# New pools for attention's tiles, other places for the next stage's first tiles, and another queue for their loads, in a two-layer metaformer on one core

## The chip, the cores and the metric

The kernel runs on one core of a Trainium2 chip. A core has five engines that run their own instruction streams and wait for each other by semaphores: TensorE (PE in the profile, its weight loads PEld), VectorE (DVE), ScalarE (ACT), GpSimd (POOL) and SyncE (SP). DMA transfers are issued from the streams of SP, ACT and POOL and are carried by 16 DMA engines. The metric is the device time of one execution in microseconds (us), the median of several runs. All data are float32.

## The reference

Four images of 384 channels and 32 x 32 positions go through two layers. Cut to what matters:

```python
x = x + attention(ln_c(x), w_qkv, w_proj, b_proj, table_q, table_k, table_v)   # 8 heads of 48
t = tokens(x)
t = t + gelu(ln(t) @ kron(c_fc_1, c_fc_2).T) @ kron(c_proj_1, c_proj_2).T
x = image(t)
x = x + convolutions(ln_c(x))          # depthwise 7x7, 5x3, 3x5, 7+7 and 5+5 separable
t = tokens(x)
t = t + mixture(ln(t), 4 experts, top 2)   # hidden 1536
x = image(t)

def attention(...):                    # n = 1024 positions; idx = clipped relative offset, 15 x 15
    a = q @ k.T * s + take(q @ table_k, idx) * s + take(k @ table_q, idx).T * s
    a = softmax(a)
    out = a @ v + scatter(a, idx) @ table_v
    return out @ w_proj + b_proj
```

## The kernel before

The kernel is written with a tile framework: a tile is taken from a pool, a pool has its place in the on-chip memory (SBUF), and the framework sets the semaphores. Pools that are opened one after the other are laid one above the other. When a stage's pools are closed, those of the next stage take the same memory, and the first instruction of each engine that uses a new pool waits for whatever still uses memory that the pool overlaps. This wait goes by pool: a tile that shares nothing with an old tile waits all the same if its pool does. The framework also orders each engine's stream; instructions passed through `pin` (`tc.keep_in_program_order`) keep the order in which they are written.

Three stages follow each other.

1. `qkv_phase` (L133) takes 512 positions at a time, eight in all. It writes `qk_d` (queries and keys) and `v_d` (values) to DRAM with DMAs that POOL issues (L179, L193). The last `v_d` store is 1 MB.

2. `attention_phase` (L199) runs over eight heads. For each head `prepare` (L294) multiplies the keys and the queries of one image column with the position tables, 32 rows in pairs: `product` gives `tabq_ps`, which ScalarE copies into a tile `st` (L318, three buffers of two rows), which SP stores in DRAM as `sd` (L319), and `tabk_ps`, which VectorE transposes into the key table `b2` (L314). For the first head nothing else goes on meanwhile. Then `fetch` (L334) reads a row of `sd` back as `s1`, and POOL adds it to a part of `b2` (L349) to make `bias`. Then come, over 32 rows of queries, scores, exponentials, transposes into `aT`, windows into `a1t`, and the products with the values `vb` and the value table `tvw`. The results go to DRAM as `ao_d`, in two halves of 16 image rows (L501), when `rd` and its spread copies `rb` (L489) have given the softmax's denominators. At the end of the last head stand `values`, four `value_table` products (`tv_ps`), `normalise` of two groups (one on VectorE, one on POOL) and `store` (L654 to L659). Before the change the pool `a_fixed` holds `vb`, `aT`, `a1t`, `tvw`, `b2` and, above these, `arow`, `extra`, `zero`, `den` and `tvs`, which are cleared by memsets when attention begins (L251 to L267). `b2` is the largest, 60 KB in each partition.

3. `rest_phase` (L902) does the projection, both feed-forward parts and the convolutions, image by image. It loads constants in three packs, on ScalarE's queue (`const`, L933): `pack0` has the projection's weights, `pack1` the first feed-forward's, among them `fold`, `pack2` the convolutions' and the gate's. `loads` (L961) brings the two halves of an image: `at` from `ao_d` and `xs`, a half of `xb`, from the input. For image 0, `at` and `xs` of half 0, then `xs` and `at` of half 1 are issued by SP. At L1441 `fold` is scaled by VectorE and centred (`sum_ps`, L128). `project` (L979) multiplies `at` with `pack0` in three chunks of 128 channels (`proj_ps`, L985) and adds to `xb` (L988), for half 0 and then for half 1; `token_stats` follows each time with `row_ps` and the statistics, `net` with the feed-forward part. The experts' first weights `w00` and `w01` are loaded on SP by `preload` (L1113) after image 0's halves, and then image 1's `xb`. `img` is cleared by POOL (L1457).

Before the change the three packs, `img` and `w` lie at the bottom of the memory (`r_w`), `xb` in `r_x` above, and `at` in `r_work`, which also holds `xc` and `scale`.

Of the kernel before, what the change touches and what calls it, by code (L numbers as in the profile page):

```python
# [11 lines left out]
F32 = mybir.dt.float32  # L12
# [6 lines left out]
P = 128  # L19
B, C, IMG = 4, 384, 32  # L20
N = IMG * IMG
NT = B * N
KC = C // P
HEADS, HD = 8, C // 8
SCALE = HD ** -0.5
MAXD = 7
SPAN = 2 * MAXD + 1
ZW = 2 * IMG - 1
NBLK = N // P
PADR = 6  # L30
AROWS = IMG + 2 * PADR
YB = 4
YT = 16
XT = 8
VW = 64
# [4 lines left out]
TOK = 512  # L40
# [27 lines left out]
WIDTHS = [sum(m for _, m in p) for p in PACKS]  # L68


def bcast(ap, dim, n):

    dims = [list(d) for d in ap.ap]
    dims[dim] = [0, n]
    return bass.AP(ap.tensor, ap.offset, dims)


def token_stats(nc, pools, ident, x, eps, rows=None, step=4):


    small, psum, tag = pools
    nj = x.shape[2] // P
    mv = small.tile([P, nj, 2], F32, tag=f"s_mv{nj}", name="s_mv")
    for j in range(nj):
        ps = psum.tile([P, TOK], F32, tag=tag, name="row_ps")
        for k in range(KC):
            nc.tensor.transpose(ps[:, k * P : (k + 1) * P], x[:, k, j * P : (j + 1) * P], ident)
        st = small.tile([P, 6], F32, tag="s_st", name="s_st")
        nc.vector.bn_stats(st, ps[:, :C])
        nc.vector.bn_aggr(mv[:, j, :], st)  # L90
        if rows is not None:
            nc.scalar.copy(rows[j], ps[:, :C])
        if j % step == step - 1:
            yield 0.7 * step, 0.45 * step
    rstd = small.tile([P, nj, 1], F32, tag=f"s_rstd{nj}", name="s_rstd")
    nc.scalar.activation(rstd, mv[:, :, 1:2], AF.Sqrt, bias=eps)
    nc.vector.reciprocal(rstd, rstd)
    return mv[:, :, 0:1], rstd


def result(steps):

    while True:
        try:
            next(steps)
        except StopIteration as end:
            return end.value


def to_partitions(nc, pools, ident, one, values):  # L110

    small, psum, tag = pools
    nj = values.shape[1]
    dg = small.tile([P, nj, P], F32, tag="s_dg", name="s_dg", bufs=1)
    nc.vector.tensor_tensor(dg, bcast(ident.unsqueeze(1), 1, nj), bcast(values, 2, P), ALU.mult)
    ps = psum.tile([P, TOK], F32, tag=tag, name="all_ps")
    nc.tensor.matmul(ps, one, dg.rearrange("p j n -> p (j n)"), start=True, stop=True)
    return ps


def center(nc, psum, tag, one, w):

    n = w.shape[2]
    for c in range(0, n, C):
        part = w[:, :, c : min(c + C, n)]
        ps = psum.tile([P, part.shape[2]], F32, tag=tag, name="sum_ps")
        for k in range(KC):
            nc.tensor.matmul(ps, one, part[:, k, :], start=(k == 0), stop=(k == KC - 1))  # L128
        for k in range(KC):
            nc.vector.scalar_tensor_tensor(part[:, k, :], ps, -1.0 / C, part[:, k, :], ALU.mult, ALU.add)  # L130
# [68 lines left out]
def attention_phase(tc, cst, held, tabs, tv, qk_d, v_d, ao_d, xs_d, heads):  # L199
# [15 lines left out]
    nc = tc.nc  # L215
# [14 lines left out]

    with ExitStack() as es:
        dram = es.enter_context(tc.tile_pool(name="a_dram", bufs=2, space=DRAM))
        fixed = es.enter_context(tc.tile_pool(name="a_fixed", bufs=1))
        work = es.enter_context(tc.tile_pool(name="a_work", bufs=2))
        small = es.enter_context(tc.tile_pool(name="a_small", bufs=4))
# [2 lines left out]
        ps_o = es.enter_context(tc.tile_pool(name="a_ps_o", bufs=1, space=PSUM))  # L238

        ident = cst["ident"]  # L240
        vb = fixed.tile([P, B, NBLK, VW], F32, name="vb")
        aT = fixed.tile([P, NBLK, YB, P], F32, name="aT")
        a1t = fixed.tile([P, 4, IMG, YT, B], F32, name="a1t")
        tvw = fixed.tile([P, 4, IMG, HD], F32, name="tvw")
        b2 = fixed.tile([P, SPAN, IMG, IMG], F32, name="b2")

        NA = 3
        arow, extra = [], []
        for i in range(NA):
# [3 lines left out]
            x = fixed.tile([P, 4, IMG], F32, name=f"extra{i}")  # L253
# [15 lines left out]
        def load_tables(h, bulk=bulk):  # L269
            for lo, i, r0 in ((64, 0, h * HD), (0, 1, C + h * HD)):  # L270
                bulk(tab[lo : lo + HD], tabs[i, h])
                yield
                for b in range(B):
                    dst, src = kq[lo : lo + HD], qk_d[r0 : r0 + HD, b * N : (b + 1) * N]
                    if lo:
                        dst = dst.rearrange("p (y b x) -> p b y x", y=IMG, b=B)[:, b]
                        src = src.rearrange("p (y x) -> p y x", x=IMG)
                    else:
                        dst = dst[:, b * N : (b + 1) * N]
                    bulk(dst, src)  # L280
                    yield
# [260 lines left out]
        for n, h in enumerate(heads):  # L542
# [27 lines left out]
            loads = iter(()) if last else load_tables(heads[n + 1])  # L570
# [331 lines left out]
def rest_phase(tc, cst, x, ao_d, ins, xs_d, y_d, x2_d, out):  # L902
# [7 lines left out]
    nc = tc.nc  # L910
    ident, one = cst["ident"], cst["one"]
    with ExitStack() as es:
        wp = es.enter_context(tc.tile_pool(name="r_w", bufs=1))
        xp_ = es.enter_context(tc.tile_pool(name="r_x", bufs=2))
        ld = es.enter_context(tc.tile_pool(name="r_ld", bufs=2))
        work = es.enter_context(tc.tile_pool(name="r_work", bufs=2))
        hid = es.enter_context(tc.tile_pool(name="r_hid", bufs=4))
        small = es.enter_context(tc.tile_pool(name="r_small", bufs=2))
# [5 lines left out]
        def pin(ins_):  # L924
            return tc.keep_in_program_order(ins_)
# [5 lines left out]
        packs = {}  # L931

        def const(name, shape):  # L933
            pack, at = PLACES[name]
            if pack not in packs:
                packs[pack] = wp.tile([P, WIDTHS[pack]], F32, name=f"pack{pack}")
                pin(nc.scalar.dma_start(packs[pack], ins[f"pack{pack}"]))
            n = int(np.prod(shape[1:]))
            t = packs[pack][:, at : at + n]
            if len(shape) == 3:  # L940
                t = t.rearrange("p (a b) -> p a b", b=shape[2])
            if len(shape) == 4:
                t = t.rearrange("p (a b c) -> p a b c", b=shape[2], c=shape[3])
            return t

        wproj = const("w_proj", [P, KC, C])
        bproj = const("b_proj", [P, KC])
        cf2 = const("c_fc_2", [P, KC])
        fold = const("fold", [P, KC, P])
        c1t = const("c_fc_1", [P, NF // 4, P])  # L950
# [6 lines left out]
        pc = {"before": const("before", [P, P]), "blocks": const("blocks", [P, MAXB]), "wrow": const("wrow", [P, 2])}  # L957
        pc["one"], pc["slot0"] = one, const("slot0", [P, NEXP])
        img = wp.tile([P, KC, IMG + 6, IMG + 6], F32, name="img")

        def loads(b, xb):  # L961

            ats = []
            for half in range(2):
                at = work.tile([P, KC, TOK], F32, tag="xc", name="at")
                xs = xb[:, :, half * TOK : (half + 1) * TOK]
                pair = [
                    (at, ao_d[half][:, b].rearrange("(k p) n -> p k n", p=P)),
                    (xs, x[b, :, half * TOK : (half + 1) * TOK].rearrange("(k p) n -> p k n", p=P)),
                ]  # L970
                for dst, src in pair[::-1] if half and not b else pair:
                    ins_ = nc.sync.dma_start(dst, src)
                    if not b:
                        pin(ins_)
                ats.append(at)
                yield 0.0, 0.0
            return ats

        def project(xs, at):  # L979

# [62 lines left out]
        def halves_of(xb):  # L1043
            return [xb[:, :, half * TOK : (half + 1) * TOK] for half in range(2)]
# [14 lines left out]
        def normalise(xb, halves, which=range(2)):  # L1059

            for half in which:
                xs = xb[:, :, half * TOK : (half + 1) * TOK]
                mean, rstd = yield from token_stats(nc, stp, ident, xs, cst["eps6"])
                mps = to_partitions(nc, (small, ps_m, "m"), ident, one, mean)
                sps = to_partitions(nc, (small, ps_m, "m"), ident, one, rstd)
                scale_sb = work.tile([P, TOK], F32, tag="scale", name="scale")
                nc.scalar.copy(scale_sb, sps)
                xc = work.tile([P, KC, TOK], F32, tag="xc", name="xc")
                nc.vector.tensor_tensor(xc, xs, bcast(mps.unsqueeze(1), 1, KC), ALU.subtract)
                halves.append((xc, scale_sb))  # L1070
                yield 3.0, 2.0
# [41 lines left out]
        def preload(w, keep=lambda ins_: ins_, which=range(2)):  # L1113
            for fh in which:
                keep(nc.sync.dma_start(w[fh], ins["w12"][fh * P : (fh + 1) * P, :]))
# [266 lines left out]
        xbs, marks = {}, {}  # L1382
# [58 lines left out]
        for k in range(KC):  # L1441
            nc.vector.tensor_scalar_mul(fold[:, k, :], fold[:, k, :], cf2[:, k : k + 1])
        center(nc, ps_m, "m", one, fold)
        xbs[0] = xp_.tile([P, KC, N], F32, name="xb", tag="xb")
        xs0, xs1 = halves_of(xbs[0])
        halves = [[] for _ in range(B + 1)]
        at0, at1 = result(loads(0, xbs[0]))
        preload(wts[0], pin)
        rstd0 = result(project(xs0, at0))
        rstd1 = result(project(xs1, at1))  # L1450
# [152 lines left out]
```

## Time and profile before

| | us |
|---|---|
| median of three runs | 3050.28 |
| lowest and highest | 3049.36, 3055.75 |
| the profiled execution | 3065.37 |
| its span, first instruction to last | 3063.6 |
| TensorE busy in it | 2923.0 (95%) |
| VectorE busy | 1960.3 (64%) |
| ScalarE busy | 1369.9 (45%) |
| GpSimd busy | 1150.8 (38%) |
| the stage of QKV ends (last `v_ps` product) at | 216.1 |
| attention's last product (`tv_ps`) ends at | 1484.0 |

The profile's times are those of one execution and count from its first instruction. A chain of waits is followed back from the last instruction: at each step to what released it, or to the instruction before it on its engine. In the timeline a line has start, length, engine, source line, operation, tiles and shapes, how many were merged, and in square brackets how long the engine was idle before and what ended that. A releaser is inferred from the semaphore that came last by the profile; where several DMAs landed together, the name can be that of a neighbour. Engine "SPq" or "ACTq" marks the issue of a DMA, not its transfer.

### The profile page before, as it was taken

Reading aid. Unit: us, or ns where it says so; the run is one execution under the profiler, and the core shown is the slowest. Engines: PE = TensorE matmul, PEld = TensorE weight load, DVE = VectorE, ACT = ScalarE, POOL = GpSimd, SP = SyncE. Lnnn points to the kernel's source line nnn. Section 1 sums busy time; section 2 is a strip of 40 time slices with the busy share of each in tenths; the row PEclk is TensorE's granted clock in tenths of the full one; section 3 lists DMA queues with packets and bytes.
Section 4 is the critical chain, followed back from the end, with each engine's and each line's share of the span. In section 5 each row is a group of like instructions: output and inputs, shape, how many; then the busy total and the mean of one; then the engine's idle time right before and its main releaser. Section 6 shows DMA issues by size and latency. Waiting matters only on the chain.

```text
span 3063.6 us, 63474 instructions
## 1 busy us (share of the span) xinstructions
PE 2923.0 (95%) x25391; PEld 2018.1 (66%) x25391; DVE 1960.3 (64%) x3577; ACT 1369.9 (45%) x2833; POOL 1150.8 (38%) x1123
## 2 busy tenths in 40 slices
PE   9988999999999999999899789999999999999996
PEld 4545777777777777777533347776577767777775
DVE  3227787878787878787478879999899540001101
ACT  1115767666766666666312232433342343233332
POOL 1114646464747473747300212251124231124412
PEclk9998999999999999999999889999999999999998
DMA  4446676767666676665400305724243165356742
GB/s 158 139 134 199 156 222 158 220 159 217 166 212 170 203 177 203 171 209 153 171 21 34 142 19 191 275 108 152 100 162 126 34 227 220 138 219 249 263 183 73
DMA packets 274568, 500.56 MB, mean 163 GB/s; under 512 B 135632, under 2 KB 204112, under 8 KB 266592
## 3 DMA queue, kind: packets, MB, share of 16 engines
q1 hardware_dynamic: 186576, 272.29, 29.0%
q0 software_dynamic: 37792, 202.68, 17.9%
q10 hardware_dynamic: 49904, 21.53, 3.6%
q8 instruction: 200, 3.28, 0.5%
q14 instruction: 96, 0.79, 0.1%
HBM read 543.58 MB, written 152.37 MB: 227 GB/s over the span
## 4 chain that ended last, share of the span: by engine, by line
PE 74%; DVE 13%; issue 6%; DMA 3%; ACT 2%; POOL 2%; SPq 0%; another core or an unknown queue 0%; DVEq 0%; POOLq 0%; ACTq 0%
PE e_ps L1309 12%; PE y_ps L1287 12%; DVE xb L1097 8%; PE t_ps L406 8%; PE sc_ps L221 7%; PE av_ps L221 7%; PE tabq_ps L221 6%; PE qk_ps L174 4%; PE a_ps L416 4%; PE tv_ps L221 2%; PE v_ps L185 2%; PE proj_ps L985 1%; PE tabk_ps L221 1%; PE tap_ps L1145 1%; PE f_ps L1020 1%
## 5 line engine op out<-in xcount | busy, mean ns | idle before, releaser
L1309 PEld LDWEIGHTS e_ps<-xT,w 128*128 128x128 f32 x4824 | 656.4, 193 | 215.1 <-issue 12.2
L349 POOL TENSOR_TENSOR bias<-b,s 128x416 f32<-128x416 f32 (+24 forms) x656 | 659.9, 1042 | 176.6 <-DMA s<-sd 160.5
L1309 PE MATMUL e_ps<-xT,w 128*128 128x128 f32 x4824 | 670.7, 277 | 11.7 <-DVE xb L1038 5.0
L1287 PE MATMUL y_ps<-w,eh 128*128 128x384 f32 x1608 | 652.4, 491 | 15.6 <-ACT eh L1312 12.8
L1097 DVE SCALAR_TENSOR_TENSOR xb<-img,pack,xb 128x1024 f32<-128x1024 f32 (+1 forms) x539 | 634.6, 1241 | 0.0
L1312 ACT ACTIVATE eh<-e_ps,w 128x128 f32<-128x128 f32 x804 | 292.8, 367 | 724.3 <-PE e_ps L1309 665.3
L1277 POOL DMA_INDIRECT w<-in_w,row x134 | 169.2, 1263 | 743.6 <-PE y_ps L1287 276.8
L398 DVE TENSOR_REDUCE extra<-arow 128x32 f32<-128x32 f32 (+24 forms) x768 | 381.7, 556 | 9.0 <-ACT arow L387 5.4
L377 DVE CUSTOM_DVE_ANT_0 arow<-sc_ps,bias 128x1024 f32<-128x1024 f32 x256 | 312.8, 1222 | 101.3 <-issue 52.5
L387 ACT ACTIVATE arow<-arow,nm 128x1024 f32<-128x1024 f32 x256 | 302.2, 1180 | 77.0 <-DVE nm L377 66.8
L406 PEld LDWEIGHTS t_ps<-ident,arow 128*128 128x128 f32 x2048 | 220.4, 142 | 173.6 <-ACT aT L407 100.6
L407 ACT COPY aT<-t_ps 128x512 f32<-128x512 f32 x512 | 278.5, 603 | 92.8 <-PE t_ps L406 91.3
L406 PE MATMUL t_ps<-ident,arow 128*128 128x128 f32 x2048 | 282.3, 281 | 15.6 <-ACT arow L387 15.6
L1290 DVE TENSOR_TENSOR yo<-y_ps,w 128x384 f32<-128x384 f32 x67 | 37.0, 553 | 394.8 <-PE y_ps L1287 389.9
L221 PE MATMUL sc_ps<-kk,qs 48*32 48x512 f32 x4096 | 277.6, 605 | 6.6 <-DVE nm L377 5.6
L1287 PEld LDWEIGHTS y_ps<-w,eh 128*128 128x128 f32 x1608 | 248.3, 193 | 30.6 <-ACT eh L1312 17.2
L221 PEld LDWEIGHTS av_ps<-aT,vb 128*64 128x64 f32 x4096 | 222.3, 137 | 51.3 <-ACT aT L407 41.2
L221 PE MATMUL av_ps<-aT,vb 128*64 128x128 f32 x4096 | 237.7, 274 | 0.0
L314 DVE STREAM_TRANSPOSE b<-tabk_ps 128x480 f32<-128x480 f32 x256 | 218.5, 982 | 23.7 <-PE tabk_ps L221 22.2
L221 PE MATMUL tabk_ps<-tab,kq 48*128 48x480 f32 x512 | 223.3, 583 | 8.2 <-DVE b L314 8.2
L221 PE MATMUL tabq_ps<-tab,kq 48*128 48x480 f32 x512 | 220.4, 579 | 2.1 <-ACT aT L407 1.5
L318 ACT COPY st<-tabq_ps 128x480 f32<-128x480 f32 x256 | 142.3, 560 | 74.8 <-PE tabk_ps L221 46.3
(210 smaller groups left out, 3140.3 us busy)
## 6 DMA issues: line engine op xcount, KB each, us to landing
sd<-st SPq DMA_DIRECT2D x128, 480.0 KB
s<-sd SPq DMA_DIRECT2D x256, 240.0 KB
xs_d<-zero SPq DMA_DIRECT2D x64, 384.0 KB
tvw<-in_tv SPq DMA_DIRECT2D x120, 192.0 KB
y_d<-yo SPq DMA_DIRECT2D x67, 192.0 KB
qk_d<-qk_sb POOLq DMA_DIRECT2D x48, 256.0 KB
qs<-qk_d SPq DMA_DIRECT2D x256, 48.0 KB
kq<-qk_d ACTq DMA_DIRECT2D x56, 192.0 KB
```

Source lines behind the costliest of these rows:

```text
L221: ins = nc.tensor.matmul(*args, **kw)
L314: turn = nc.vector.transpose(b2.rearrange("p e y x -> p x (e y)")[:, i + j], ps[:, j, : SPAN * IMG])
L349: nc.gpsimd.tensor_tensor(bias[:, y0:y1, :], bass.AP(b2.tensor, b2.offset + (e * IMG + y0) * IMG, [list(b2.ap[0]), [(step * IMG + 1) * IMG ...
L377: nc.vector.tensor_tensor_reduce(s["flat"], ps.rearrange("p h n -> p (h n)"), s["bias"].rearrange("p y x -> p (y x)"), -SCALE, BIG, ALU.ad ...
L387: nc.scalar.activation(s["flat"], s["flat"], AF.Exp, bias=s["nm"], scale=-1.0, accum_out=dn[:, y % YT : y % YT + 1])
L398: pin(nc.vector.tensor_reduce(ex[:, i, :], a[:, p0:p1, :].rearrange("p y x -> p x y"), AX.X, ALU.add))
L406: pin(nc.tensor.transpose(pt[:, j, :], s["flat"][:, k0 : k0 + P], ident))
L407: pin(nc.scalar.copy(aT[:, 4 * g : 4 * g + 4, s["y"] % YB, :], pt))
L1097: ins_ = nc.vector.scalar_tensor_tensor(acc[:, k, y0:y1], img[:, k, dy + y0 : dy + y1, dx : dx + IMG], w7[:, k, dy, dx : dx + 1], acc[:, k ...
L1287: nc.tensor.matmul(py, hs, w[:, o : o + C], start=(ff == 0), stop=(ff == NF - 1))
L1309: nc.tensor.matmul(ph, w[:, o : o + P], xT[k][:, c, :], start=(c == 0), stop=(c == KC - 1))
L1312: nc.scalar.activation(hs, ph, AF.Gelu, bias=w[:, o : o + 1])
```

## The change

Attention's pool `a_fixed` is divided in three. `a_late` takes `vb`, `aT`, `a1t` and `tvw`, `a_table` takes `b2`, and `a_fixed` keeps the tiles that are cleared by memsets. In the rest, `at` and `xc` go from `r_work` to a pool `r_xc` of their own, the packs from `r_w` to a new pool `r_p`, and the pool of gathered rows, `r_ld`, is opened before `r_x`. With that the two `xb` tiles, `at`, `xc` and the packs lie in the memory that `b2` had. `loads` for image 0 is called right after `pack0` has been issued, and all of its transfers but the last (`at` of half 1) are issued by ScalarE. The packs `pack1` and `pack2` follow on the same queue.

```diff
+        late = es.enter_context(tc.tile_pool(name="a_late", bufs=1))
+        table = es.enter_context(tc.tile_pool(name="a_table", bufs=1))
         fixed = es.enter_context(tc.tile_pool(name="a_fixed", bufs=1))
...
-        vb = fixed.tile([P, B, NBLK, VW], F32, name="vb")
-        aT = fixed.tile([P, NBLK, YB, P], F32, name="aT")
-        a1t = fixed.tile([P, 4, IMG, YT, B], F32, name="a1t")
-        tvw = fixed.tile([P, 4, IMG, HD], F32, name="tvw")
-        b2 = fixed.tile([P, SPAN, IMG, IMG], F32, name="b2")
+        vb = late.tile([P, B, NBLK, VW], F32, name="vb")
+        aT = late.tile([P, NBLK, YB, P], F32, name="aT")
+        a1t = late.tile([P, 4, IMG, YT, B], F32, name="a1t")
+        tvw = late.tile([P, 4, IMG, HD], F32, name="tvw")
+        b2 = table.tile([P, SPAN, IMG, IMG], F32, name="b2")
...
         wp = es.enter_context(tc.tile_pool(name="r_w", bufs=1))
+        ld = es.enter_context(tc.tile_pool(name="r_ld", bufs=2))
         xp_ = es.enter_context(tc.tile_pool(name="r_x", bufs=2))
-        ld = es.enter_context(tc.tile_pool(name="r_ld", bufs=2))
+        xcp = es.enter_context(tc.tile_pool(name="r_xc", bufs=2))
+        pp = es.enter_context(tc.tile_pool(name="r_p", bufs=1))
...
-                packs[pack] = wp.tile([P, WIDTHS[pack]], F32, name=f"pack{pack}")
+                packs[pack] = pp.tile([P, WIDTHS[pack]], F32, name=f"pack{pack}")
...
         bproj = const("b_proj", [P, KC])
+        def loads(b, xb):
...
+                at = xcp.tile([P, KC, TOK], F32, tag="xc", name="at")
...
+                for i, (dst, src) in enumerate(pair):
+                    if b:
+                        nc.sync.dma_start(dst, src)
+                    else:
+                        pin((nc.scalar if i or not half else nc.sync).dma_start(dst, src))
...
+        xb0 = xp_.tile([P, KC, N], F32, name="xb", tag="xb")
+        at0, at1 = result(loads(0, xb0))
         cf2 = const("c_fc_2", [P, KC])
...
-                for dst, src in pair[::-1] if half and not b else pair:
-                    ins_ = nc.sync.dma_start(dst, src)
-                    if not b:
-                        pin(ins_)
...
-                xc = work.tile([P, KC, TOK], F32, tag="xc", name="xc")
+                xc = xcp.tile([P, KC, TOK], F32, tag="xc", name="xc")
...
-        xbs[0] = xp_.tile([P, KC, N], F32, name="xb", tag="xb")
+        xbs[0] = xb0
...
-        at0, at1 = result(loads(0, xbs[0]))
```

In the stream of TensorE the order changes in one place: the first two chunks of half 0's projection stand before the sum of `fold`, where before only the first product did. On SP, `xb` of image 1 stands ahead of the last two stores of `ao_d`, where before it came after `w00` and `w01`. The memsets of `arow`, `extra`, `zero`, `tvs` and `den` stand at the start of the program. The other instructions of every engine keep their order, apart from a few small ones of VectorE next to the projection.

More of the change, by code (lines that the diff above doesn't have):

```diff
@@ L947, in rest_phase @@
         bproj = const("b_proj", [P, KC])
+        def loads(b, xb):
+            ats = []
+            for half in range(2):
+                at = xcp.tile([P, KC, TOK], F32, tag="xc", name="at")
+                xs = xb[:, :, half * TOK : (half + 1) * TOK]
+                pair = [
+                    (at, ao_d[half][:, b].rearrange("(k p) n -> p k n", p=P)),
+                    (xs, x[b, :, half * TOK : (half + 1) * TOK].rearrange("(k p) n -> p k n", p=P)),
+                ]
+                for i, (dst, src) in enumerate(pair):
[3 more added lines that the diff above has]
+                        pin((nc.scalar if i or not half else nc.sync).dma_start(dst, src))
+                ats.append(at)
+                yield 0.0, 0.0
+            return ats
+        xb0 = xp_.tile([P, KC, N], F32, name="xb", tag="xb")
+        at0, at1 = result(loads(0, xb0))
         cf2 = const("c_fc_2", [P, KC])
@@ L959, in rest_phase @@
         img = wp.tile([P, KC, IMG + 6, IMG + 6], F32, name="img")
[L961 to L970, printed above, removed]
-                for dst, src in pair[::-1] if half and not b else pair:
-                    ins_ = nc.sync.dma_start(dst, src)
-                    if not b:
-                        pin(ins_)
-                ats.append(at)
-                yield 0.0, 0.0
-            return ats
         def project(xs, at):
```

## The prediction

> **What bounds the kernel now.** I read the page first: its chain of waits, then the stretches between the three stages in the chain in order of time, then the same stretches in the timeline, where the square bracket gives the idle time before an instruction and what ended it.
>
> ```profile
> span 3063.6 us, 63474 instructions
> ...
> PE 74%; DVE 13%; issue 6%; DMA 3%; ACT 2%; POOL 2%; SPq 0%; another core or an unknown queue 0%; DVEq 0%; POOLq 0%; ACTq 0%
> ```
>
> TensorE carries three quarters of the chain, and inside a stage the change does not touch it. So only TensorE's holes at the two seams can move: QKV to attention (216 to 260 us) and attention to the rest (1477 to 1506 us). The timeline of the first seam:
>
> ```profile
> 217.28 0.91 POOL L193 DMA_DIRECT2D v_d<-va  x1 [7.38 <-ACT va L188]
> ...
> 227.46 1.27 POOL L251 MEMSET arow<- 128x1408 f32 x1 [9.28 <-DMA sd<-st]
> 227.47 0.13 DVE L261 MEMSET den<- 128x32 f32 x2 [18.40 <-DMA sd<-st]
> 227.51 3.52 DVE L314 STREAM_TRANSPOSE b<-tabk_ps 128x480 f32<-128x480 f32 x4
> ...
> 229.39 1.17 PE L221 MATMUL tabk_ps<-tab,kq 48*128 48x480 f32 x1 [8.23 <-DVE b L314]
> ```
>
> VectorE sits for 18.4 us before two memsets of 0.13 us that nobody needs yet. The page names `sd<-st`, but in the program `den`'s memset waits for the QKV stage's last stores, among them `v_d` (issued 217.28; its semaphore reaches its value at 226.75), because `den` shares the pool `a_fixed` with tiles that lie in QKV's memory. The table transposes (L314) stand behind it, `tabk_ps` runs out of banks, and TensorE stands still for 8.23 us. The second seam, as a chain:
>
> ```profile
> 1476.59 7.38 PE tv_ps L221 x256
> ...
> 1484.82 8.72 DMA pack<-in_pack
> 1493.55 0.03 issue
> 1493.57 0.30 DVE pack L1442
> 1493.87 0.04 issue
> 1493.91 1.65 PE sum_ps L128 x6
> 1495.56 7.81 PE proj_ps L985 x16
> ```
>
> and the same seam as windows (busy time of PE, PEld, DVE, ACT, POOL, then the granted clock, the DMA share and GB/s):
>
> ```profile
> 1470.00:1484.00 14.00, 13.13 (x336) 12.53 (x336) 7.35 (x21) 4.07 (x10) 0.00 (x0) 1.00 0.13 41
> 1484.00:1495.00 11.00, 3.13 (x7) 1.66 (x8) 4.39 (x12) 0.00 (x0) 4.93 (x2) 0.64 0.85 307
> 1495.00:1510.00 15.00, 14.37 (x41) 6.96 (x41) 7.12 (x23) 1.58 (x2) 14.70 (x22) 0.92 1.02 413
> ```
>
> The DMA engines idle (0.13) while TensorE does the last value table; all loads of the next stage start at 1484, and TensorE works 3.1 of the next 11 us.
>
> **What the Trainium skill says.** "TensorE: Matmul & The Clock Gate", section "What's actually happening": after a free-running window of some 3.4 us without work the array runs at half rate until a busy window has passed. The trace agrees: after the 8.23 us hole a table product's chain share is 0.79 us, from 234.5 on 0.40. "DMA: Bandwidth & Descriptors", section "Queues, rings and completion order": the engines go round the queues that have work, and within a ring descriptors are taken in order. So a queue's first transfer is not held by its later ones, but two busy queues share. The trace agrees in that `pack0` on ScalarE's queue landed at 1490.65 beside `at` and `x` on SP's. I use no price of the skill.
>
> **The change, part by part** (times are those of before).
>
> *Nothing is added but two memsets moved.* Instruction counts are equal; of 23,074 instructions 72 have other waits, all at the two seams or in which DMA semaphore a later load uses. Attention's tiles keep their addresses; only the pools they wait as are new.
>
> *First seam: `arow`, `extra`, `zero`, `tvs`, `den` no longer wait.* Their memsets (POOL 3x1.27 + 3x0.20 + 0.42 + 0.31 = 5.1 us, DVE 0.13) move to the start. `arow0`'s now stands ahead of `ident`'s select (done at 1.31 us), which becomes some 2.6 to 3.5; the first transpose waits for `xt` until 5.36, and POOL's first `qk_d` issue comes over 10 us later. Cost 0, at worst 0.3. `b2` is now a pool of its own, above QKV's memory, so L314 waits only for VectorE's and ScalarE's last QKV operation (216.7). `aT`, `a1t`, `vb` still wait for `v_d`; first used after 260, so free.
>
> What is late next? TensorE needs 4 records of 0.2 us = 0.81 us a row for 32 rows. Rows 0 to 8 run from 216.75 to 224.0. Then the store `sd<-st` decides: `st` has three buffers of two rows, so row 6's copy waits for the first store, which lands at 226.92 behind `kk` and `v_d`. The three banks of `ps_t` let TensorE get to row 8, so it stops from 224.0 to 227.5 (226.95 + 0.56). Rows 9 to 31 then take 23 x 0.81 = 18.6, and the last copy ends near 246.7 instead of 255.50: 8.8 us. Against it: the 3.5 us hole may fill a clock window (half rate for a window, some 1.7 us), and in the trace one store landed late (254.40, a stall of 1.33); counted again, the gain is 7.5. From there, fetch, bias and scores follow with the same waits. I take 8.0; bounds 5 (cold clock and late stores) and 9.3.
>
> *Second seam: who can start when.* `pack0`, `at` and `x` of image 0 and the other packs now lie in `b2`'s memory, free since POOL's last bias sum (1460.8). ScalarE issues them behind its last copy (L440, 1476.64 + 0.37): `pack0` at 1477.05, then `at`, both halves of `x`, `pack1`, `pack2`, at about 0.45 each, the last two when the `rb` loads have landed (1479.8). Nothing stands behind them on ScalarE until the root at 1507. On SP, image 1's two `x` loads (0.79 MB each), before behind the weights `w`, now go right after `rb` at 1476.7 and 1478.0, ahead of the `ao_d1` stores: they share the engines with ScalarE's queue. That is the hidden price.
>
> Bytes: two `x` of image 1, `pack0` 0.59, `at` 0.79, two `x` 1.57, `pack1` 0.79 MB: 5.3 MB until `pack1` is in. At 370 GB/s (the DMA view of the seam, in 40 slices, has 310 to 440 once filled) from 1478.5: 14.3 us, landing at about 1492.8. `pack0` and `at` come first: with half of the engines about 1485, so TensorE waits for about 1 us after 1484 instead of 6.9, does two chunks of the projection (12 records x 0.43 = 5.2, to some 1490.5) and then stands before the sum of `fold`, which needs `pack1`. So `pack1` still ends the wait, hardly earlier than before (1493.55). But behind it there are now 6 records of projection, not 16. Sum from 1493.1 to 1494.5, third chunk 2.6: 1497.1, against 1503.37. Gain 6.2.
>
> Second half: `ao_d1`'s store waits, as before, for POOL's product behind the memset of `img` (done 1489.1). SP's queue is empty by then, the store lands near 1492.3, `at` of half 1 is issued then and is there at about 1496.8; it is needed at 1497.1 + 2.4 = 1499.5. 2.7 us of cover. I take 6.0; bounds 2 (`pack1` at 1495 with a cold clock) and 8.5 (`pack1` at 1490.5).
>
> *After that* everything hangs on the second half's chain (root, `net`, taps, the convolution on VectorE), and `w`, image 1's loads and POOL's diagonals come as early or earlier, so the shift is carried to the end.
>
> Sum: -8.0 - 6.0 = -14.0 us. The profiled execution (3065.37 with what lies around its span of 3063.6) would go to 3051.4; the median of 3050.28, whose run is 0.5% shorter, to **3036.3**.
>
> **The rivals.**
> 1. *The first seam pays, the second hardly.* Image 1's loads push `pack1` to 1496 or so and TensorE is cold behind it: 2 from the second seam, 7 from the first: 3041. For it: ScalarE's queue has `pack1` fifth, and the first of them, 2 KB rows for the most part, ran at 310 to 410 GB/s, not 430. Against: `pack0` in its larger rows got more than its half in 1488 to 1493.
> 2. *The first seam is replaced by the stores.* Three `st` buffers and stores of 2.4 to 4.5 us keep the tables at the stores' pace, 2 us gained there and 6 at the second seam: 3042. Against: from 232 to 252 the stores kept up with 0.81 us a row.
> 3. *It does nothing measurable:* the two holes are refilled at a later common wait. I find none: no step is paced by absolute time. About 3047 to 3053.
> 4. *Slower: image 1's loads ahead of everything.* If the mix at the second seam ran at R GB/s, the third chunk would end at 1478.5 + 5300/R + 4.3. It equals 1503.37 at R = 258; at R = 150 the seam costs 15 us, and with 8 from the first the kernel takes 3057. It decides below about 190. For it: six loads and two stores at once on two queues. Against: no slice with such loads in flight ran under 310.
>
> **How the numbers follow.** Chances: forecast 0.64, rival 1 0.17, rival 2 0.08, rival 3 0.07, rival 4 0.04. The range goes from both upper bounds, less a little (-17.5, with some luck of clock windows -20: 3030), to rival 2 with some noise of clock windows, 3044.5; rivals 3 and 4 stay outside, and some of the tails. About 0.2%, 6 us, is what can be told from no change here: faster 0.88, same 0.08, slower 0.04.
>
> **What would show it.** In the changed profile: VectorE's 18.4 us before `den` gone and its first table transpose before 219; TensorE's hole at 220 to 229 down to 3 to 4 us, ended by a copy that waits for `sd<-st`; the first score product 7 to 9 us earlier. At the second seam the DMA share high already from 1478 (less the shift), the wait for `pack` after `tv_ps` near 1 us, and a second wait of 2 to 4 us before `sum_ps`. The prediction is wrong if `at` of half 1 or `pack1` is late by more than 3 us, if stores pace the table rows, or if a load of image 1 is what `proj_ps` waits for.

## The result, and the profile after

| | before | after |
|---|---|---|
| median of 12 runs each, us | 3052.68 | 3040.39 |
| lowest and highest after | | 3034.25, 3047.69 |
| ratio, with its 95% interval | | 0.9963 (0.9954 to 0.9973) |
| profiled execution (span) | 3065.37 (3063.6) | 3037.78 (3036.0) |
| TensorE busy in it | 2923.0 (95%) | 2914.2 (96%) |

The change is worth 0.0037 x 3052.7 = 11.3 us (the recorded ratio is not that of the two medians, which lie 12.3 apart). Forecast were 14 and 3036.3 us; with nine more runs the median of before itself rose from 3050.28 to 3052.68. The page of the kernel after begins, and sums its chain of waits, with:

```profile
span 3036.0 us, 63460 instructions
...
PE 74%; DVE 11%; issue 8%; DMA 3%; POOL 2%; ACT 2%; SPq 0%; ACTq 0%; POOLq 0%; DVEq 0%
```

TensorE still carries three quarters of the chain. The first seam in the timeline of the kernel after (start, length, engine, line, operation, in brackets the idle time before and what ended it):

```profile
218.62 0.90 POOL L193 DMA_DIRECT2D v_d<-va  x1 [7.38 <-ACT va L188]
...
219.55 7.56 DVE L316 STREAM_TRANSPOSE b<-tabk_ps 128x480 f32<-128x480 f32 x9 [9.14 <-PE tabk_ps L221]
...
227.89 2.39 ACT L320 COPY st<-tabq_ps 128x480 f32<-128x480 f32 x4 [3.99 <-DMA sd<-st]
...
228.51 0.77 PE L221 MATMUL tabq_ps<-tab,kq 48*128 48x480 f32 x1 [2.59 <-ACT st L320]
```

VectorE's 18.4 us before `den` are gone: it starts the transposes at 219.55, as soon as TensorE delivers. What is late next is `st`: ScalarE waits 3.99 us for the first store `sd<-st`, and TensorE stands still for 2.59 us behind it instead of 8.23. The second seam in the chain of the same execution:

```profile
1475.54 14.39 DMA pack<-in_pack
1489.93 0.03 issue
1489.95 0.30 DVE pack L1449
1490.25 0.04 issue
1490.30 0.94 PE sum_ps L128 x6
1491.23 2.59 PE proj_ps L992 x6
```

and in its timeline:

```profile
1471.84 2.81 SPq L964 DMA_DIRECT2D xb<-in_x  x2
1472.28 1.04 ACTq L966 DMA_DIRECT2D at<-ao_d  x1
...
1482.62 7.08 PE L992 MATMUL proj_ps<-at,pack 128*128 128x512 f32 x12 [3.52 <-DMA at<-ao_d]
...
1490.30 0.94 PE L128 MATMUL sum_ps<-pack,one 128*128 128x128 f32 x6 [0.60 <-DVE pack L1449]
```

The loads are issued while the last value table runs (it ends at 1479.09), and two chunks of the projection now stand before the sum. But TensorE waits 3.52 us for `at`, not 1, and does those 12 records in 7.08 us; the same 12 took 5.39 us in another run. The last wait of the seam is still that for `pack1` (0.60 us before `sum_ps`). Image 1's `xb` on SP (first line) is issued at the same moment as the first loads of image 0.

The two profiled spans differ by 27.6 us, more than twice the result. ScalarE's 2,797 operations (its table loads left out) are the same in every kernel of this study, so two traces can be laid over each other one by one. Counted from QKV's last copy (`va`), half 1's projection comes 10.9 us earlier after (1278.6 against 1289.5). From there to the end the two traces differ by 18 us more, 13.4 of them between 2750 and 2950 us, where TensorE works for the experts. The windows of 2700 to 2950 us (busy time of PE, PEld, DVE, ACT, POOL with counts, clock, DMA share, GB/s), first of before:

```profile
2700.00:2950.00 250.00, 238.73 (x1439) 188.32 (x1437) 33.15 (x61) 77.80 (x203) 88.45 (x90) 0.98 0.60 214
```

of after:

```profile
2700.00:2950.00 250.00, 246.15 (x1523) 195.58 (x1522) 34.44 (x63) 82.90 (x214) 91.31 (x93) 1.00 0.64 232
```

and of a kernel that has the first part of the change (the first experiment below):

```profile
2700.00:2950.00 250.00, 239.36 (x1457) 189.88 (x1457) 34.06 (x62) 79.07 (x205) 88.78 (x90) 0.99 0.61 219
```

That kernel has the change's gain and still the slow experts: it ran on a chip on which the kernel before takes 3065.6 us, where it takes 3050.9 and 3049.2 on the chip of the later runs. In this window TensorE is busy for 238.6 to 240.0 us in all four traces from the first of these chips and for 246.14 or 246.15 in all seven from the other, whatever the kernel. So this part of the difference goes with the chip, not with the change; why the chips differ is open. Spans are compared below only up to half 1's projection, and times only as ratios within one chip.

### The profile page after: what moved, and what is told of

It is laid out like the page before. It is cut to its first block, busy times and chain, and to the rows that moved or that the text cites. A ratio compares the mean times of both kernels' runs of the same rounds, so it can differ in the third digit from the quotient of the medians.

```text
span 3036.0 us, 63460 instructions
## 1 busy us (share of the span) xinstructions
PE 2914.2 (96%) x25391; PEld 2017.5 (66%) x25391; DVE 1960.5 (65%) x3577; ACT 1370.9 (45%) x2833; POOL 1156.4 (38%) x1123
## 4 chain that ended last, share of the span: by engine, by line
PE 74%; DVE 11%; issue 8%; DMA 3%; POOL 2%; ACT 2%; SPq 0%; ACTq 0%; POOLq 0%; DVEq 0%
PE e_ps L1316 14%; PE y_ps L1294 13%; PE t_ps L408 7%; PE av_ps L221 7%; PE sc_ps L221 7%; DVE xb L1104 6%; PE tabq_ps L221 5%; PE qk_ps L174 4%; PE a_ps L418 3%; PE v_ps L185 2%; PE tv_ps L221 2%; PE tap_ps L1152 1%; DVE extra L400 1%; PE row_ps L87 1%; POOL bias L351 1%
## 5 line engine op out<-in xcount | busy, mean ns | idle before, releaser
L221 PEld LDWEIGHTS tabq_ps<-tab,kq 48*128 48x128 f32 x512 | 148.6, 296 | 44.4 <-ACT aT L409 5.4
```

The source lines that it names most:

```text
L221: ins = nc.tensor.matmul(*args, **kw)
```

## The experiments

Eleven runs, in three groups: e1 to e4 on one chip, e5 to e8 and later e9 to e11 on another. The changed kernel ran in the last two groups, so that e2 to e4 are compared with it through the kernel before. Each trace gives three lengths: from the start of QKV's last `va` copy to the end of the last table copy (first seam), from the end of the last `tv_ps` to half 1's projection (second seam), and from `va` to half 1's projection. Ratios are to the kernel before on the same chip.

| kernel | tables | second seam | va to half 1 | ratio (95%) |
|---|---|---|---|---|
| before | 39.4 | 21.7 | 1289.5 | 1 |
| changed | 32.3 | 17.0 | 1278.6 | 0.9963 (0.9954-0.9973) |
| changed (e5) | 34.3 | 18.5 | 1283.8 | 0.9962 (0.9947-0.9977) |
| changed (e9) | 32.2 | 17.7 | 1282.1 | 0.9968 (0.9952-0.9983) |
| attention's pools only (e1) | 32.5 | 17.9 | 1280.6 | 0.9959 (0.9943-0.9974) |
| the same (e6) | 33.7 | 19.1 | 1284.6 | 0.9967 (0.9955-0.9980) |
| `den` with the late tiles (e2) | 39.5 | 18.1 | 1290.4 | 0.9991 (0.9983-1.0000) |
| image 1 behind the weights (e3) | 33.9 | 12.7 | 1275.8 | 0.9958 (0.9942-0.9974) |
| the same (e10) | 32.7 | 12.8 | 1273.8 | 0.9956 (0.9941-0.9971) |
| five tiles `st` (e4) | 27.6 | 16.6 | 1275.3 | 0.9945 (0.9930-0.9960) |
| both edits (e7) | 27.8 | 15.9 | 1272.8 | 0.9940 (0.9926-0.9953) |
| both, `img` in its own pool (e8) | 27.5 | 12.9 | 1269.2 | 0.9929 (0.9915-0.9942) |
| the same (e11) | 27.9 | 12.9 | 1274.2 | 0.9941 (0.9925-0.9956) |

The two seams repeat within 1 or 2 us. What lies between them, attention's heads, varies by up to 5 us from run to run (1228.3 to 1233.4), which is why the third column scatters.

**Attention's pools alone (e1, e6).** The kernel before with the first part of the diff (lines of `late`, `table`, `fixed`); the rest keeps its packs, places and queues.

> Only attention's pool is divided in three; the rest of the kernel is that of before, with its packs, loads and places. Theory (two independent seams, 7.1 us from the first and 4.6 from the second, as the two traces read): the first seam's gain alone, 5.5 to 8.5 us, ratio about 0.9977; VectorE's first table transpose within 3 us of QKV's last copy. Rival (the first seam's gain is filled up again at a later common wait, and the second seam carries the result): 0 to 2 us, ratio 0.9995 or more.

Measured: the first seam as expected, but the ratio is that of the whole change. Neither theory said that. The timeline of e1 at the second seam tells why:

```profile
1471.88 7.53 PE L221 MATMUL tv_ps<-a1t,tvw 128*48 128x64 f32 x256
1472.19 0.54 SPq L974 DMA_DIRECT2D at<-ao_d  x1
1472.78 1.32 SPq L974 DMA_DIRECT2D xb<-in_x  x1
...
1479.57 1.53 ACTq L939 DMA_DIRECT2D pack<-in_pack  x3
...
1483.78 2.04 PE L987 MATMUL proj_ps<-at,pack 128*128 128x512 f32 x2 [4.37 <-DMA pack<-in_pack]
```

In the old layout, too, `xb` and `at` share no memory with the tiles that the last value table reads, and only the common pool kept them back: with `b2` in a pool of its own SP issues `at` and half 0 of `x` at 1472, 7 us before the table ends; only the packs, at the bottom of the memory, wait for it. With 1.6 MB already in or on its way, `pack1` takes 5.57 us and not 8.72. So the first part of the diff pays at both seams. To set a price on the second part, the whole change and e1's kernel were run side by side.

> The changed kernel itself, beside its first part alone on the same chip. Theory (dividing attention's pool already lets SP start image 0's loads early, so that new places and ScalarE's queue bring about 1 us, which the trace has: 17.1 us from the last value table's end to half 1's projection against 18.0): within 2 us of the first part alone. Rival (the second seam brings the 4.6 us that the first pair of traces showed): 4 us or more faster than the first part alone.

> Only attention's pool divided in three, again. Theory: ratio within 0.0006 of that of the changed kernel run beside it, and at and x of image 0 are issued by SP before the last value table ends, the packs after it. Rival: the ratio is higher by 0.0013 or more.

Measured: 0.9962 and 0.9967, 0.0005 (1.5 us) apart with intervals of 4 us to either side, medians 3.8 us apart, and second seams of 18.5 and 19.1 us. The times alone don't tell 1 us from 4; with e1 (0.9959) and the other two runs of the changed kernel the mean ratios are equal to 0.0001. In the means of the traces the second part of the diff is worth 0.9 us at the seam (five traces of the changed second seam, 17.0, 18.5, 17.7, 18.1 and 16.6, against 17.9 and 19.1). The theory of about 1 us holds there; 4.6 us for this part falls. But the 0.9 us are what is left of two effects: in e1 image 1's `xb` is loaded behind `w00` and `w01`, in the changed kernel ahead of them. The runs e3 and e10 below part the two.

**`den` alone (e2).**

```diff
-            d = fixed.tile([P, IMG], F32, name=f"den{i}")
+            d = late.tile([P, IMG], F32, name=f"den{i}")
```

> The changed kernel with one edit: den's two tiles of 128 bytes a partition are taken from the pool of vb, aT, a1t and tvw, so that their two memsets of 0.13 us on VectorE wait again for the QKV stage's last stores. Theory (these memsets alone held the table transposes): VectorE's 18 us before den are back, TensorE's hole before the tables is back near 8 us, and of the 11.3 us only the second seam's 4 to 6 are left, ratio about 0.9983. Rival (it was the whole pool with b2, POOL's memsets or the stores that held the tables): the time stays at that of the changed kernel, ratio 0.9963.

```profile
228.43 0.12 DVE L263 MEMSET den<- 128x32 f32 x2 [18.25 <-DMA sd<-st]
228.47 3.37 DVE L316 STREAM_TRANSPOSE b<-tabk_ps 128x480 f32<-128x480 f32 x4
...
230.29 1.17 PE L221 MATMUL tabk_ps<-tab,kq 48*128 48x480 f32 x1 [8.02 <-DVE b L316]
```

The timeline of e2 has the stall of before to within 0.2 us: 18.25 before the memset, 8.02 before TensorE, tables 39.5 us. All else is the changed kernel. Two tiles of 128 bytes a partition, in a pool that waits, are enough to hold the whole seam, with POOL's memsets and `b2` already free. It does not follow that `den` alone held it before: `b2` stood in the same pool then, its transposes would by the rule of pools have waited without `den` too, and no run moves `den` alone. The ratio, 0.9991, is a gain of 2.7 us, less than the 4 to 6 expected of the second seam.

**Five tiles for the first stores (e4).** For the first head only, two of every five `st` take the place of `oT`, unused there.

```diff
-                st = work.tile([P, 2, SPAN * IMG], F32, tag="bias", name="st", bufs=3)
+                more = h == heads[0] and i // 2 % 5 > 2
+                st = work.tile(
+                    [P, 2, SPAN * IMG], F32, tag="o" if more else "bias", name="st", bufs=2 if more else 3
+                )
```

> The changed kernel with five tiles st for the first tables instead of three: two of every five take the place of oT, which is not in use there. Theory (the hole of 2.6 us in the tables, and the half clock behind it, come from the copy of row 6 that waits for the first sd store): the hole is gone and the tables end 3 to 4.5 us earlier, ratio about 0.9951. Rival (the stores, late behind v_d and kk, set the pace, or the last store and fetch do): the hole moves to row 10 or the end, under 1.5 us more than the changed kernel, ratio 0.9958 or above.

```profile
219.54 26.64 DVE L319 STREAM_TRANSPOSE b<-tabk_ps 128x480 f32<-128x480 f32 x32 [9.14 <-PE tabk_ps L221]
```

All 32 transposes now follow each other without a gap (in the changed kernel 9, and then pieces). The tables end 4.6 to 6.7 us earlier than in the changed kernel, more than the 3 to 4.5 expected. In the changed kernel's first trace the hole of 2.59 us was followed by 3.41 us at a granted clock of 0.50 (230.06 to 233.47), which is 1.7 us lost, 4.3 in all; in e5 the hole was 3.14 us and the half clock lasted 6.83. In e4 the clock is 1.00 throughout the tables. The row-6 wait is shown to be what was left of the first seam; stores that set the pace of the rows are excluded.

**Image 1 behind the weights (e3, e10).** The two `xb` loads of image 1 are issued right after `preload(wts[0], pin)`; only SP's order changes.

```diff
         preload(wts[0], pin)
+        xbs[1] = xp_.tile([P, KC, N], F32, tag="xb", name="xb")
+        for half, xs in enumerate(halves_of(xbs[1])):
+            src = x[1, :, half * TOK : (half + 1) * TOK]
+            pin(nc.sync.dma_start(xs, src.rearrange("(k p) n -> p k n", p=P)))
```

> The changed kernel with the two loads of image 1's x (0.79 MB each) moved on SP behind the weights w00 and w01, where they stood before; no other instruction moves. Theory (these 1.57 MB share the DMA engines with pack0 and at and make the 3.5 us wait for at, the half clock behind it and the late pack1): at lands before the last value table ends, no wait of TensorE for it, second half of the projection 5 to 7 us earlier, ratio about 0.9943. Rival (at and pack1 are late because of their place in ScalarE's queue, or at of half 1 ends the wait next): under 2 us more than the changed kernel, ratio 0.996 or above.

Measured: at the seam nearly the theory, in the time neither. The timeline of e3:

```profile
1471.73 7.53 PE L221 MATMUL tv_ps<-a1t,tvw 128*48 128x64 f32 x256
1472.01 0.37 ACTq L941 DMA_DIRECT2D pack<-in_pack  x1
1472.42 1.03 ACTq L966 DMA_DIRECT2D at<-ao_d  x1
...
1479.34 0.67 PE L992 MATMUL proj_ps<-at,pack 128*128 128x512 f32 x1
1481.31 4.88 PE L992 MATMUL proj_ps<-at,pack 128*128 128x512 f32 x11 [1.30 <-issue]
...
1486.12 0.93 PE L128 MATMUL sum_ps<-pack,one 128*128 128x128 f32 x6
```

No wait for `at`, a granted clock of 1.00, no wait before the sum: `pack1` is in 6.5 us after the value table instead of 10.8, and the second seam takes 12.7 us instead of 17.6. With its repetition below (12.8) that is also 5.7 us less than with attention's pools alone (e1, e6): so much the new places and ScalarE's queue bring at the seam, and image 1's early loads take 4.8 of it back. Yet the ratio was 0.9958. It was run again beside the changed kernel.

> The changed kernel beside the next two on one chip, since the run with image 1 behind the weights had a trace that was 4.8 us better at half 1's projection and a median that was not. Every theory: ratio 0.9962, give or take 0.001.

> The changed kernel with image 1's x behind w00 and w01, again. Theory (the 4.8 us that the traces show from the last value table's end to half 1's projection reach the end): 3 to 5.5 us less than the changed kernel beside it, ratio 0.9944 to 0.9952. Rival (they are given back where image 1's x is now late, or the good trace was chance): under 2 us less, and the trace has no half 1 earlier than 15.5 us after the last value table, or a wait for xb later that the changed kernel does not have.

Measured: 0.9968 and 0.9956, 3.7 us apart with intervals that overlap, and a second seam of 12.8 us again. Laid over each other by ScalarE's instructions, e10 has 4.9 us at half 1's projection, loses 1.6 of them near 1580, has lost 4.1 by 1715, and is down by 2.0 from 1748 to 2700. The chain of e9 in that stretch:

```profile
1586.50 1.93 PE tap_ps L1152 x13
...
1713.20 5.51 DMA xb<-in_x
```

and that of e10:

```profile
1578.56 3.27 PE tap_ps L1152 x13
```

The same 13 taps take 1.93 us in one and 3.27 in the other, at a granted clock of 0.50 from 1577.95 to 1581.37 where it is 1.00 in e9 (e3 has the same stretch, from 1578.88); and the wait of 5.51 us for a later `xb`, on the chain of e9, is not on that of e10. So 2 of the 4.9 us are given back, partly to a colder clock; 2.9 should remain, which fits the 2.1 us between the mean ratios (0.9957 against 0.9964). The 3.7 us of e10 alone lie in the theory's 3 to 5.5, both pairs together don't. A loss behind the seam is there, as the rival said, but it takes less than half, and not by the wait that the rival named, which e10 has not.

**Both edits (e7), and `img` apart (e8, e11).** e7 joins the two edits. In e8 and e11 `img` is moreover taken from a pool opened before `r_w`:

```diff
+        ip = es.enter_context(tc.tile_pool(name="r_i", bufs=1))
         wp = es.enter_context(tc.tile_pool(name="r_w", bufs=1))
...
-        img = wp.tile([P, KC, IMG + 6, IMG + 6], F32, name="img")
+        img = ip.tile([P, KC, IMG + 6, IMG + 6], F32, name="img")
```

> The changed kernel with both edits: five tiles st for the first tables, and image 1's x behind w00 and w01. Theory (two seams that don't depend on each other): 3.4 us from the first and 3 to 4.4 us from the second, 6 to 8 us less than the changed kernel, from the last copy of va to half 1's projection about 1271 us against 1278.7. Rival (what is won at the first seam is lost at the second, or the other way round): under 4 us less than the changed kernel.

> The kernel with both edits and img in a pool of its own, which overlaps no tile that the last value table reads: POOL can clear img before that table ends, and its product before the last store of ao_d is not behind the memset. Theory (in the run with image 1 behind the weights, at of half 1 landed 0.16 us ahead of half 1's projection, so it does not yet set the end): within 1 us of the kernel without this edit, with at of half 1 landing 1.5 to 3.5 us earlier against the projection. Rival (at of half 1 is what half 1 waits for): 1.5 us faster or more.

> Both edits and img's own pool, again. Theory (5.8 us from the tables, 4.8 us from the loads): 8 to 11 us less than the changed kernel beside it, ratio 0.9926 to 0.9936, and half 1's projection 12 to 13.5 us after the last value table. Rival (the two gains overlap): under 6 us less.

Measured: e7 0.9940, 6.7 us under the changed kernel beside it. The sum was as expected, its terms were not: 5.1 us came from the tables and 1.7 from the second seam, which kept 15.9 us. e8 is 3.4 us below e7 by the ratios and 2.3 by the medians, with overlapping intervals, where 1 was expected; `at` of half 1 was in time in both (1.9 and 0.5 us ahead), so the rival's reason is excluded, and the theory's, that `at` would come earlier against the projection, did not come true either. What differs is what follows the first record of the projection, in e7

```profile
1474.26 0.67 PE L995 MATMUL proj_ps<-at,pack 128*128 128x512 f32 x1 [1.03 <-DMA at<-ao_d]
1477.02 6.58 PE L995 MATMUL proj_ps<-at,pack 128*128 128x512 f32 x11 [2.10 <-issue]
```

and in e8:

```profile
1473.46 0.67 PE L996 MATMUL proj_ps<-at,pack 128*128 128x512 f32 x1 [0.93 <-DMA at<-ao_d]
1474.39 4.88 PE L996 MATMUL proj_ps<-at,pack 128*128 128x512 f32 x11 [0.27 <-issue]
```

In e7 there is a hole of 2.10 us, for which the profile shows no wait, and behind it a granted clock of 0.50 for 3.41 us (from 1477.16); in e8 neither. In e3, e7 and e10 POOL's memset of `img` (3.71 us) runs during that hole, which is 1.30 to 2.10 us; in e8 and e11 it is over before, and the hole is 0.27 and 0.45. The memset is not shown to be the cause: in e5 the first records also run under it (1484.70, memset until 1485.32) without a hole. Nor is a gain of `img`'s own pool shown: e3 and e10 have the memset, the hole and no half clock, and their seams of 12.7 and 12.8 us are as short as the 12.9 of e8 and e11. e11 gave 0.9941, by the ratios 8.2 us under the changed kernel beside it, which is in the expected 8 to 11, and by the medians 5.3, which is not; the ratio expected was not met. The two runs with all three edits have a mean ratio of 0.9935, about 9 us below the changed kernel; e7 without the last edit is not told apart from them.

## Why the prediction was right, and where its terms were off

The result (3040.39) lies in the range, on the side forecast, 4 us above the point, and 2.4 of these 4 are the higher median of before. As a number it is nearer to the first two rivals (3041 and 3042), so it does not speak for the forecast by itself. By the traces the seams gave 6.3 and 4.1 us, where the forecast had 8 and 6, the first rival 7 and 2, and the second 2 and 6: the second is out, and the result lies between the forecast and the first. By the prediction's own steps:

- *The memsets move at no cost, `b2` no longer waits.* Right. TensorE's first instruction starts at 5.36 us before and at 5.36 to 5.68 in the twelve other traces, so the memsets cost 0.3 us at most. e2 shows that `den`'s two are enough to hold the tables.
- *Row 6's copy waits for the first store, TensorE's hole shrinks to 3.5 us.* Right in kind: 2.59 us, ended by that copy. The gain of 8.0 was too large: the tables ended 5.1 to 7.2 us earlier in the seven traces with three `st` tiles and the divided pool (mean 6.3). The mis-sized term is rows 9 to 31 with the last copy: 19.2 us were forecast (227.5 to 246.7), and from the end of the hole to the last copy it was 21.2 (228.51 to 249.73). Of the 2.0 us 1.7 are the half clock behind the hole (0.50 for 3.41 us), which the prediction named but counted only in small part. A late store, its other reserve, cost little: of the three traces of the change only that of e5 has a second wait for a store, 0.75 us.
- *ScalarE's queue and the new places let the loads start before the table ends.* This step failed as an attribution. `b2`'s own pool alone releases `at` and the first half of `x`, on SP and in the old places (e1). The prediction compared the two layouts only, and didn't ask what each single pool would release. Of the 6.0 us counted for the second seam, image 1's loads included, 3.2 came with attention's pools alone (21.7 to 18.5) and 0.9 with the second part of the diff: 5.7 that its places and queue bring, less 4.8 for image 1's loads.
- *The second seam is worth 6.0.* It went from 21.7 us to 17.6 in the mean of five traces: 4.1. The terms: the wait for `at` was put at 1 us and is 3.52, 3.19 and 4.15 in the three traces of the change; `pack1` was put at 8.8 us after the value table (1492.8 - 1484.0) and landed 10.8 after it (1489.93 - 1479.09). It is `pack1` that counts: TensorE waits for it last in all three traces (0.60, 2.44 and 0.85 us before `sum_ps`), so that the longer wait for `at` is covered. These 2.0 us too many are the mis-sized term of the seam. They lie between the forecast and the first rival, which put `pack1` 3 us later than the forecast (1496 or so, not 1492.8). The rate was nearly right: the window of 1479 to 1490 us, in the columns above, reads

```profile
1479.00:1490.00 11.00, 7.18 (x16) 2.79 (x12) 4.42 (x11) 0.00 (x0) 4.93 (x2) 0.84 0.98 373
```

  The bytes were not. From the first issue plus 1.5 us, as the prediction counted, to 1489.93 the DMA engines took 16.6 us and moved 362 GB/s, 6.0 MB, where 5.3 MB were counted. What was left out can only be from the `rb` copies (4 x 0.13 MB, the last landing at 1475.55), `pack2` (0.3 MB) and `ao_d1`'s stores (2 x 0.2 MB), of which a part falls into this stretch.
- *Image 1's loads are the hidden price.* Right in kind, and now with its number: 4.8 us at the seam, about 2 to 3 at the end (e3, e10). The wait of `proj_ps` for `at` is theirs, since it is gone in e3; that comes close to the last of the prediction's signs of being wrong. 1.57 MB at 373 GB/s are 4.2 us.
- *`at` of half 1 is in time, and the shift is carried to the end.* Right. In after it landed at 1494.91, 1.2 us before it was needed, and from half 1's projection up to 2450 us the trace of after stays within about 2 us of that of before (those of e5 and e9 within about 5).
- *Sum.* 6.3 and 4.1 us are 10.4; the ratios of the three groups with the changed kernel give 11.3, 11.6 and 9.8. Both terms were too large, by a fifth and by a third.

On the clock the Trainium skill ("TensorE: Matmul & The Clock Gate", section "What's actually happening") says that its window of some 3.4 us runs free, so the same hole can cost differently from run to run. The traces agree: each of the three traces of the change has one stretch of 3.41 us at a granted clock of 0.50 in the second seam, but in those of after and e9 it lies in the 12 records behind `at` (7.08 and 6.85 us, behind holes of 3.52 and 4.15), and in e5 (5.39, behind 3.19) it comes only at 1493.68, behind the wait for `pack1`. The start of the program shows the free beat best: TensorE begins at 5.36 to 5.68 us in all thirteen traces, the clock goes to 1.00 anywhere between 8.25 (e11) and 11.60 (after), and QKV's last copy comes at 216.11 in the one and 217.46 in the other. The section also puts the slow clock behind an idle window of this length; here, by the records of the traces, a shorter hole was enough, 2.53 us before the half clock in the first seam of e9 and 2.59 in that of after, and the measurement decides. A forecast of one value for such a term can be off by the 1.7 us that one such stretch costs.

## What to carry to other kernels

Where waits go by pool, list for each pool of the next stage which old pools it overlaps, and ask this of every part of a change alone: a pool divided for one seam can release loads at another, and a memset of 0.13 us in the wrong pool can hold an engine for 18. When a load is made earlier, add up all bytes in flight until the one that is waited for, spread copies and stores among them, and keep what is not needed soon off the queues: at this seam the early loads of image 1 took back 4.8 of the 5.7 us that the new places and the second queue won.

## What the runs showed of the hardware

Some operations of VectorE and GpSimd stand in each other's way. `begin` (L858), a VectorE operation on 128x4 values, takes 1.35 us when POOL clears `img`, in the timeline of e7, and the product of `oT` and `rb` before it 0.69:

```profile
1473.34 3.71 POOL L1470 MEMSET img<- 128x4332 f32 x1 [23.16 <-PE tv_ps L221]
...
1474.97 0.69 DVE L504 TENSOR_TENSOR oT<-oT,rb 128x512 f32<-128x512 f32 x1
...
1475.72 1.35 DVE L858 TENSOR_SCALAR begin<-done 128x4 f32<-128x4 f32 x1
```

`begin` ends at 1477.07, and the memset at 1477.05. In e8 the memset is done before, and POOL works on its own half of `oT` beside VectorE:

```profile
1474.23 1.26 POOL L504 TENSOR_TENSOR oT<-oT,rb 128x512 f32<-128x512 f32 x1 [19.76 <-DVE count L1196]
1474.26 1.78 DVE L504 TENSOR_TENSOR oT<-oT,rb 128x512 f32<-128x512 f32 x1
...
1476.10 0.17 DVE L858 TENSOR_SCALAR begin<-done 128x4 f32<-128x4 f32 x1
```

Now `begin` takes 0.17 us, and VectorE's operation on `oT` 1.78 instead of 0.69. The Trainium skill ("SBUF — State Buffer", section "SBUF: two separate sides") calls the port pair that the two engines share an exclusive lock for a whole instruction, and names who takes it: GpSimd, and of VectorE's operations those in a mode that uses both ports, or with two inputs in SBUF, these only against a GpSimd operation that reads SBUF. The traces agree: the operation with two inputs is not held by the memset, which reads nothing, and is held by POOL's operation, which reads; the one with a single input is held by the memset, although no trace shows its mode. e11 has the same 1.78 and 0.17 us. The delays cost nothing here, since nothing waits for `begin` and `at` of half 1 is still 0.5 us ahead in e8, but they show why a small VectorE operation can look eight times as long as it is.
